# Selective scan: sums kept by columns, and running sums added by VectorE as it empties the bank

## The chip, the cores and the metric

The kernel runs on one core of one Trainium2 chip. A core has five engines that run their own instruction streams and wait for one another through semaphores: TensorE (PE; its weight loads are listed apart as PEld), VectorE (DVE), ScalarE (ACT), GpSimd (POOL) and SyncE (SP), which here only issues DMAs. The metric is the time of one execution on the device in microseconds; less is better. All data are float32.

## The reference

The model has two layers on an input x of shape (4, 384, 32, 32), that is 4 batches of 384 channels on a 32 x 32 picture.

Layer 0 normalises x in 32 groups of channels and runs a selective scan over the pixels in four directions k: 0 by rows, 1 by columns, 2 by rows backwards, 3 by columns backwards. Each of the 384 channels has 16 states:

```python
def step(h, inp):
    dtt, ut, bt, ct = inp
    dA = jnp.exp(dtt[..., None] * A)
    h = h * dA + (dtt * ut)[..., None] * bt[:, :, None, :]
    y = jnp.einsum('bkdn,bkn->bkd', h, ct)
    return (h, y)
```

The results of the four directions are added per pixel, those of 1 and 3 after being turned from column order to row order, and so is D * u. A layer norm over channels, a GELU and a residual follow.

Layer 1 turns the picture into 1024 tokens of 384 channels per batch: layer norm, attention with 6 heads in a causal window of 64, a projection, a residual; then a layer norm and a mixture of 4 experts (384 to 1536 to 384, exact GELU), of which each token uses its two best, and a last residual.

## The kernel before, in words

**How the order of the work is made.** The program is written as generators: one for each stage, each yielding one operation after another, or a condition to wait for. The class Machine runs them while the program is built. It keeps a clock for each engine, gives each operation a cost (`Engine.ask`, lines 155 to 199), and always issues the operation that could start first, with a bias: EARLY (-6 us) for the scan's surroundings and attention, LATER (+6 us) for the experts. So the order of the instructions on each engine is fixed when the program is built and follows from these costs; the chip only waits where data are not ready. `Engine.run` issues one operation, `Engine.all` several as one (line 144). For TensorE the costs are stretched by COLD = 1.9[...]; an operation marked `steady` is not stretched. The helpers record almost every instruction under two lines, L142 (single operations) and L153 (those issued together), so the profile is read by the names of tiles.

**The scan.** There are 16 turns: 4 batches, in each the directions 1, 3, 0, 2 (ORDER). A turn has 12 blocks of 32 channels, and a block has 4 groups of 4 states, so that a tile holds 32 channels x 4 states on 128 partitions and 1024 pixels along the free axis: 48 tiles a turn, 768 in all. Two blocks are worked side by side. For each tile:

- `times_b`: GpSimd multiplies dt * u (dts) by B (bc) into a tile z, one of seven;
- `decay`: ScalarE writes dA = exp(dt * A) into one of two tiles in PSUM;
- `scan`: VectorE runs the recurrence (TENSOR_TENSOR_SCAN), in place in dA or into z;
- `times_c`: VectorE (z<-dA,bc) or GpSimd (z<-z,bc) multiplies by C. The planner chooses by which of the two clocks is behind.

**The sum over states, and over directions.** `fold_y` (line 873) is where the change lies. For each pair of blocks it takes a tile yp of 128 x 512 (two blocks x two halves of 32 channels on the partitions, 512 pixels along), loads what the earlier directions have summed so far from ydr in HBM, takes one of three PSUM banks (ps_y), and puts yp into it by a matmul with the identity. Then, for each of the four groups of states, it adds the two z tiles: a matmul with the weights `fold` (128 x 32, adding the four states of each channel) for each half of 512 pixels, so four matmuls, which the profile lists as eight instructions, on four strips of 32 columns of the array. For directions 1 and 3 the z tile is in column order, and the fold reads it so that the result comes out in row order: 32 neighbouring results take every 32nd element of z. ScalarE copies the bank back to yp and it is stored in ydr. There are 96 such calls. z tiles go back to `times_b` when their fold has been issued. The first value in ydr is D * u (yd), written by `normal` in `group_norm`, line 667.

**The rest.** When the 48 folds of all directions of a batch are through, `tokens` does the attention in 8 tiles of 128 tokens, `route` picks experts and gives each token a row, GpSimd scatters the rows by indirect DMA, and `experts` works 19 blocks of 128 rows per batch (76 in all). A block is 36 matmuls ps_hid, 36 GELUs on ScalarE, 12 matmuls y_ff and 3 transposes ps_xb (the profile shows two instructions for each matmul), and loads 8 tiles of weights of 576 KB. `combine` gathers the two rows of a token and adds them. The experts of one batch run beside the scan of the next; those that are not done when the scan of the last batch ends follow after it.

Of the kernel before, what the change touches and what calls it, by code (L numbers as in the profile page):

```python
# [12 lines left out]
AF = mybir.ActivationFunctionType  # L13
ALU = mybir.AluOpType
# [4 lines left out]
B, D, HH, WW = 4, 384, 32, 32  # L19
# [12 lines left out]
NG = NS // SG  # L32
# [78 lines left out]
class Op:  # L111


    def __init__(self, eng, outs, ins, cost, table, size):
        self.eng, self.outs, self.ins, self.cost, self.table, self.size = eng, outs, ins, cost, table, size
        self.work = 0.0
        self.steady = False


TABLES = {AF.Exp: "exp", AF.Ln: "ln", AF.Gelu: "gelu", AF.Sqrt: "sqrt"}  # L120
# [10 lines left out]
class Engine:  # L131
# [12 lines left out]
    def all(self, calls):  # L144

        asked = [self.ask(*c) for c in calls]
        outs, ins = ([ap for o in asked for ap in getattr(o, side)] for side in ("outs", "ins"))
        whole = Op(self.name, outs, ins, sum(o.cost for o in asked), None, 0)
        whole.work = sum(o.work for o in asked)
        whole.steady = asked[-1].steady  # L150
        yield whole
        for op, a, k in calls:
            getattr(self.real, op)(*a, **k)  # L153

    def ask(self, op, a, k):
        aps = [v for v in list(a) + [v for n, v in k.items() if n not in ("out", "accum_out")] if hasattr(v, "tensor")]
        if "out" in k:
            outs, ins = [k["out"]], aps
        else:
            outs, ins = aps[:1], aps[1:]  # L160
        if op == "value_load":
            outs, ins = [], aps
        if op == "tensor_tensor_reduce":
            outs, ins = outs + ins[-1:], ins[:-1]
        if k.get("accum_out") is not None:
            outs = outs + [k["accum_out"]]
        for v in list(k.values()):
            if isinstance(v, bass.IndirectOffsetOnAxis):
                ins = ins + [v.ap]
        n = max(v.free_size() if callable(v.free_size) else v.free_size for v in (outs if op == "matmul" else outs + ins))  # L170
        size, table = 0, None
        if "dma" in op:
            size = max(_nbytes(v) for v in outs + ins[:1])
            if op == "indirect_dma_start":
                size = P * D * 4
            cost = dict(pool=1.0, act=0.38, sp=0.48)[self.name]
        elif self.name == "pe":
            cost = max(n, 90) * (0.00088 if op == "transpose" else 0.00176)
            if outs[0].shape[0] == 32:
                cost = 0.108 + 0.000417 * n  # L180
            if ins[0].shape[0] < 32:
                cost *= 0.6
        elif self.name == "act":
            cost = 0.08 + 0.00085 * n + 0.1 * sum(hasattr(k.get(v), "tensor") for v in ("bias", "scale"))
            cost += 0.19 if "accum_out" in k else 0.0
            table = TABLES.get(a[2]) if op == "activation" else None
        elif self.name == "pool":
            cost = 0.1 + 0.0022 * n
        elif self.name == "sp":
            cost = 1.5  # L190
        else:
            cost = 0.17 + 0.00198 * n if "scan" in op else 0.14 + 0.00105 * n
            if n < 256 and not any(v.space == PSUM for v in outs + ins):
                cost += 0.5
        asked = Op(self.name, outs, ins, cost, table, size)
        if self.name == "pe":
            asked.steady = outs[0].shape[0] == 32
            asked.work = cost * min(ins[0].shape[0], P) / P if outs[0].shape[0] > 32 else 0.5 * cost
        return asked


def _nbytes(ap):
    n = 4
    for s in ap.shape:
        n *= s
    return n
# [6 lines left out]
class Machine:  # L213
# [50 lines left out]
    def account(self, op, start):  # L264
        e = op.eng
        if op.table and op.table != self.table:
            start += TABLE_LOAD
            self.table = op.table
        end = start + op.cost
        if e == "pe":  # L270

            left, end = op.cost, start
            while left > 0:
                n = int(end / WINDOW)
                f = 1.0 if op.steady or self.worked.get(n - 1, 0.0) > WINDOW / 3 else COLD
                step = min(left * f, (n + 1) * WINDOW - end + 1e-6)
                self.worked[n] = self.worked.get(n, 0.0) + op.work * step / f / op.cost
                left, end = left - step / f, end + step
        self.busy[e] += end - max(self.clock[e], start)
        self.clock[e] = end  # L280
        if op.size:
            self.dma = max(self.dma, end) + op.size / DMA_RATE
            end = max(end + DMA_TIME, self.dma + 1.0)
            e = "dma"
        for aps, log, w in ((op.ins, self.read, False), (op.outs, self.written, True)):
            for ap in aps:
                name = ap.tensor.name
                if str(ap.space) .endswith("DRAM"):
                    self.dram.setdefault(name, []).append((*self.span(ap), end, w))
                elif log.get(name, (0.0, None))[0] <= end:  # L290
                    log[name] = end, e
        self.reach = max(self.reach, end)
# [80 lines left out]
WINDOW, COLD = 3.413, 1.9  # L373
# [5 lines left out]
def conv_attn_hybrid(  # L379
# [29 lines left out]
    ident = const.tile([P, P], F32, name="ident")  # L409
# [5 lines left out]
    dsum = const.tile([P, T], F32, name="dsum")  # L415
    nc.vector.tensor_reduce(dsum, ds_sb.rearrange("p k t -> p t k"), AX.X, ALU.add)

    fold = const.tile([P, 32], F32, name="fold")
# [55 lines left out]
    with tc.tile_pool(name="setup", bufs=1) as setup:  # L474
# [15 lines left out]
        for j in range(JB):  # L490
            ps = banks.now("ps_al")
# [44 lines left out]
    pwl = dram.tile([P, T * D], F32, name="pwl", bufs=1)  # L536

    ORDER = (1, 3, 0, 2)
    turns = [(b, ORDER[ki]) for b in range(B) for ki in range(KG)]
    blocks = [(i, t, j) for i in range(len(turns)) for t in range(T) for j in range(JB)]  # L540
    NSLOT = len(blocks) * NG
# [7 lines left out]
    pe, act, dve, pool, sp = m.pe, m.act, m.dve, m.pool, m.sp  # L549
# [65 lines left out]
    def group_norm(b):  # L615
# [17 lines left out]
        g = rp.tile([P, 5, T], F32, tag="g", name="g", bufs=1)  # L633
# [3 lines left out]
        ps = yield from banks.take("ps_gm", 0)  # L637
        for n, src in enumerate((mean, dev)):
            for t in range(T):
                yield from pe.matmul(  # L640
                    ps[:GROUPS, T : T + 1], gm[:, t, :], src[:, t : t + 1],
                    start=t == 0, stop=t == T - 1,
# [16 lines left out]
        def normal(t):  # L659
            u = yield from us_.take("un")  # L660
            yield from sp.dma_start(u, x[b, ts(t, P)].rearrange("p h w -> p (h w)"))
            yield from act.activation(
                u, u, AF.Identity, bias=g_off[:, t : t + 1], scale=g_rstd[:, t : t + 1]
            )
            yield from sp.dma_start(udr[b][t], u)
            yd = yield from zs_.take("yd")
            yield from act.activation(yd, u, AF.Copy, scale=dsum[:, t : t + 1])
            us_.give(u)
            for j in range(JB):
                yield from sp.dma_start(  # L670
                    ydr[b][t, j].rearrange("(q d) l -> d q l", q=2),
                    yd[32 * j : 32 * j + 32, :].rearrange("d (q l) -> d q l", q=2),
                )
            zs_.give(yd)
# [198 lines left out]
    def fold_y(n):  # L873


        i, t, j = blocks[n]
        b, k = turns[i]
        rows_y = ydr[b][t, j : j + 2].rearrange("j r l -> (j r) l")
        prev = yield from yps.take("yp")
        yield from sp.dma_start(prev, rows_y)  # L880
        ps = None
        for g in range(NG):
            s = n // 2 * SP + 2 * g
            yield lambda: s in ready and s + 1 in ready
            pair = zs[s], zs[s + 1]
            yield m.settled(*pair)
            mm = Calls()
            if ps is None:
                ps = yield from banks.take("ps_y", 0)
                mm.matmul(ps, ident, prev, start=True, stop=False)  # L890
            for n_z, z in enumerate(pair):
                for h in range(2):
                    if k % 2:
                        rhs = z.rearrange("p (w h) -> p h w", h=HH)[:, ts(h, HH // 2), :]
                    else:
                        rhs = z[:, ts(h, LH)]
                    q = 32 * (2 * n_z + h)
                    mm.matmul(ps[q : q + 32, :], fold, rhs, start=False, stop=g == NG - 1)
            yield from pe.all(mm)
            zs_.give(zs.pop(s), zs.pop(s + 1))  # L900
        yield from act.copy(prev, ps)
        banks.give(ps)
        yield from sp.dma_start(rows_y, prev)
        yps.give(prev)
        folded[b] = folded.get(b, 0) + 2
        if folded[b] == KG * NB:
            have.add(("scan", b))
# [601 lines left out]
```

## Time and profile before

| | |
|---|---|
| three runs, median (lowest to highest) | 4246.56 us (4246.25 to 4254.88) |
| profiled execution | 4255.8 us |
| its span, first to last instruction | 4254.0 us |
| mean granted TensorE clock | 0.819 |
| busy PE, DVE, ACT, POOL | 3377.0, 2852.8, 2373.1, 2813.7 us |
| first scan, last fold, end | 103, 3175, 4254 us |
| fold matmuls / identity matmuls (instructions) | 3072, mean 914 ns / 192, mean 814 ns |
| copies yp<-ps_y on ScalarE | 96, mean 584 ns |

The page gives the busy time of each engine over the whole span, which is a sum over stages that have different limits; the view by windows gives the same for stretches of time. A line of a group reads: source line, engine, operation, output<-inputs, shapes, count, busy time, mean duration of one in ns, then the idle time of the engine just before them and what ended it. In a timeline a line gives the start in us, the duration in us, the engine, the source line, the operation and how many were merged; what stands in brackets is the idle time before it. PEclk is the clock that TensorE was granted, 1.0 being full speed.

### The profile page before, as it was taken

The numbers are of one execution on the slowest core, as the hardware profiler recorded it, in microseconds if no ns is written. First come the engines' busy times: TensorE is split into PE (matmuls) and PEld (weight loads), VectorE is DVE, ScalarE is ACT, GpSimd is POOL, SyncE is SP. The second block draws the span as 40 slices with busy tenths as digits, with TensorE's granted clock in tenths as the row PEclk, the third lists the DMA queues.
The fourth block names the chain that finished last, engine by engine and source line by source line (L and its number), as shares of the span: only waits on it lengthen the run. The fifth ranks groups of instructions, "written<-read, shape, count | busy, mean of one in ns | idle before, by whom it ended". The sixth has DMA issues, their size and how long they took to land. (4 is left out here: it accounts for less than half of the span.)

```text
span 4254.0 us, 50073 instructions
## 1 busy us (share of the span) xinstructions
PE 3377.0 (79%) x16222; PEld 1952.7 (46%) x16222; DVE 2852.8 (67%) x2995; ACT 2373.1 (56%) x3961; POOL 2813.7 (66%) x1468
## 2 busy tenths in 40 slices
PE   2556555588875987978788787887899999999997
PEld 1000110144441553534445343444567777887875
DVE  2999999987888978888888888888861222001001
ACT  2555455666655887777677767677663443222221
POOL 1999989997897899988878889898871001101001
PEclk7655665687875998878788887887899999999997
DMA  6566563542446985635668846556577438998995
GB/s 210 200 239 230 202 227 127 177 150 107 150 145 240 365 326 189 221 124 195 211 232 293 297 149 205 187 189 216 176 248 260 138 103 301 355 319 294 313 319 165
DMA packets 368573, 935.16 MB, mean 220 GB/s; under 512 B 48372, under 2 KB 160120, under 8 KB 368312
## 3 DMA queue, kind: packets, MB, share of 16 engines
q1 hardware_dynamic: 360120, 906.79, 61.3%
q0 software_dynamic: 8192, 25.17, 1.7%
q8 instruction: 129, 2.11, 0.2%
q14 instruction: 132, 1.08, 0.1%
HBM read 786.39 MB, written 164.30 MB: 223 GB/s over the span
## 5 line engine op out<-in xcount | busy, mean ns | idle before, releaser
L142 POOL TENSOR_TENSOR z<-dts,bc 128x1024 f32<-128x1024 f32 x768 | 1796.2, 2364 | 236.5 <-PE ps_y L153 136.9
L142 ACT ACTIVATE dA<-dts,a 128x1024 f32<-128x1024 f32 x768 | 853.1, 1118 | 488.6 <-DVE z L142 467.6
L153 PE MATMUL ps_y<-z,fold 128*32 128x512 f32 x3072 | 827.1, 914 | 320.8 <-DVE z L142 162.8
L142 DVE TENSOR_TENSOR_SCAN dA<-dA,z 128x1024 f32<-128x1024 f32 x414 | 947.3, 2288 | 111.1 <-ACT dA L142 92.1
L142 POOL TENSOR_TENSOR z<-z,bc 128x1024 f32<-128x1024 f32 x354 | 831.1, 2360 | 101.0 <-DVE z L142 100.1
L142 DVE TENSOR_TENSOR_SCAN z<-dA,z 128x1024 f32<-128x1024 f32 x354 | 795.7, 2276 | 55.7 <-ACT dA L142 53.1
L153 PEld LDWEIGHTS ps_hid<-xbt,w_sb 128*128 128x128 f32 x5472 | 683.4, 201 | 136.5 <-issue 22.4
L153 PE MATMUL ps_hid<-xbt,w_sb 128*128 128x128 f32 x5472 | 702.0, 286 | 40.7 <-ACT dt L142 16.4
L153 PE MATMUL y_ff<-w_sb,hs 128*128 128x384 f32 x1824 | 664.4, 503 | 14.3 <-ACT hs L142 7.9
L142 ACT ACTIVATE hs<-ps_hid,bb 128x128 f32<-128x128 f32 x912 | 271.9, 366 | 542.2 <-PE ps_hid L153 417.3
L142 DVE TENSOR_TENSOR z<-dA,bc 128x1024 f32<-128x1024 f32 x414 | 505.9, 1222 | 23.3 <-PE ps_y L153 0.5
L153 PEld LDWEIGHTS ps_y<-z,fold 128*32 128x32 f32 x3072 | 93.9, 122 | 800.7 <-POOL z L142 336.5
L142 ACT ACT_TABLE_LOAD x340 | 436.2, 1283 | 12.0 <-PE ps_g L153 5.8
L153 PEld LDWEIGHTS y_ff<-w_sb,hs 128*128 128x128 f32 x1824 | 333.4, 196 | 228.0 <-issue 40.3
L142 POOL DMA_INDIRECT cb<-ysdr,idx x64 | 61.8, 966 | 548.8 <-DMA cb<-t2dr 269.7
L153 POOL TENSOR_TENSOR rn<-rn,half 128x1 f32<-128x1 f32 x96 | 52.6, 548 | 288.6 <-DVE rn L153 286.6
L142 DVE COPY xbt<-ps_xb 128x384 f32<-128x384 f32 x40 | 22.2, 556 | 329.2 <-PE ps_xb L153 329.2
L153 PE MATMUL ps_y<-yp,ident 128*128 128x512 f32 x192 | 139.1, 814 | 90.0 <-ACT yp L142 20.9
L142 POOL DMA_INDIRECT xsdr<-tks,idx x64 | 63.7, 995 | 208.5 <-DMA xsdr<-tks,idx 151.3
L153 PE MATMUL ps_o<-v,pt 128*128 128x64 f32 x720 | 160.1, 345 | 6.1 <-ACT dt L142 2.3
L142 DVE COPY yb<-y_ff 128x384 f32<-128x384 f32 x27 | 15.0, 556 | 214.4 <-PE y_ff L153 205.1
L153 PEld LDWEIGHTS ps_o<-v,pt 128*128 128x128 f32 x720 | 130.1, 228 | 43.7 <-ACT dt L142 4.0
(187 smaller groups left out, 3480.3 us busy)
## 6 DMA issues: line engine op xcount, KB each, us to landing
w_sb<-wl SPq DMA_DIRECT2D x608, 576.0 KB
dts<-dtr SPq DMA_DIRECT2D x384, 512.0 KB
bc<-xdr SPq DMA_DIRECT2D x128, 512.0 KB
ub<-udr SPq DMA_DIRECT2D x48, 512.0 KB
dtr<-e SPq DMA_DIRECT2D x48, 512.0 KB
dtr<-dt SPq DMA_DIRECT2D x48, 512.0 KB
yp<-ydr SPq DMA_DIRECT2D x96, 256.0 KB
ydr<-yp SPq DMA_DIRECT2D x96, 256.0 KB
```

What stands on the lines that cost most here:

```text
L142: return getattr(self.real, op)(*a, **k)
L153: getattr(self.real, op)(*a, **k)
```

## The change

The sums in ydr are kept in column order for as long as directions 1 and 3 run, and yp no longer goes through TensorE.

- `normal` writes the first yd in column order: ScalarE reads u by columns and writes yd contiguously, as two halves of 16 rows, each by columns.
- For directions 1 and 3 the fold reads z as it lies: of each picture column a run of 16 pixels (a half of the picture) and then the next column's run. The result is in column order.
- The first matmul of the bank is now that of the first group (start where g == 0), not the identity.
- After the last group VectorE adds the bank to yp, into yp, instead of ScalarE's copy.
- In direction 3, the last by columns, ScalarE then writes yp back into the bank in row order and copies the bank to yp, so that directions 0 and 2 and `tokens` find row order. This holds for 24 of the 96 calls.
- In the planner the mark `steady` goes, the cost of a fold matmul is 0.01 + 0.00022 n instead of 0.108 + 0.000417 n (for n = 512: 0.123 us instead of 0.321), stretched by COLD like any other, and several operations issued together take the activation table of the first that has one. The planner's new costs change the order of instructions on every engine.

```diff
 class Op:
         self.work = 0.0
-        self.steady = False
...
     def all(self, calls):
-        whole = Op(self.name, outs, ins, sum(o.cost for o in asked), None, 0)
+        table = next((o.table for o in asked if o.table), None)
+        whole = Op(self.name, outs, ins, sum(o.cost for o in asked), table, 0)
         whole.work = sum(o.work for o in asked)
-        whole.steady = asked[-1].steady
...
             if outs[0].shape[0] == 32:
-                cost = 0.108 + 0.000417 * n
+                cost = 0.01 + 0.00022 * n
...
         if self.name == "pe":
-            asked.steady = outs[0].shape[0] == 32
...
-                f = 1.0 if op.steady or self.worked.get(n - 1, 0.0) > WINDOW / 3 else COLD
+                f = 1.0 if self.worked.get(n - 1, 0.0) > WINDOW / 3 else COLD
...
     ORDER = (1, 3, 0, 2)
+    LAST_BY_COLUMNS = 3
...
         def normal(t):
-            yield from act.activation(yd, u, AF.Copy, scale=dsum[:, t : t + 1])
+            yield from act.activation(
+                yd.rearrange("p (q w h) -> p q w h", q=2, w=WW),
+                u.rearrange("p (q h w) -> p q w h", q=2, w=WW), AF.Copy, scale=dsum[:, t : t + 1],
+            )
...
     def fold_y(n):
             if ps is None:
                 ps = yield from banks.take("ps_y", 0)
-                mm.matmul(ps, ident, prev, start=True, stop=False)
             for n_z, z in enumerate(pair):
                 for h in range(2):
                     if k % 2:
-                        rhs = z.rearrange("p (w h) -> p h w", h=HH)[:, ts(h, HH // 2), :]
+                        rhs = z.rearrange("p (w h) -> p w h", h=HH)[:, :, ts(h, HH // 2)]
                     else:
                         rhs = z[:, ts(h, LH)]
                     q = 32 * (2 * n_z + h)
-                    mm.matmul(ps[q : q + 32, :], fold, rhs, start=False, stop=g == NG - 1)
+                    mm.matmul(ps[q : q + 32, :], fold, rhs, start=g == 0, stop=g == NG - 1)
             yield from pe.all(mm)
             zs_.give(zs.pop(s), zs.pop(s + 1))
-        yield from act.copy(prev, ps)
+        yield from dve.tensor_tensor(prev, ps, prev, ALU.add)
+        if k == LAST_BY_COLUMNS:
+            yield from act.copy(
+                ps.rearrange("p (h w) -> p w h", w=WW), prev.rearrange("p (w h) -> p w h", w=WW)
+            )
+            yield from act.copy(prev, ps)
         banks.give(ps)
```

## The prediction

> **What bounds the kernel now.** I read the summary by stages first, because a busy share over the whole span mixes stages with different limits. The window view gives the busy time of each engine in each stretch, then the granted TensorE clock, the DMA share and GB/s:
>
> ```profile
> core 0: us, PE busy (x) PEld busy (x) DVE busy (x) ACT busy (x) POOL busy (x), PEclk, DMA share, GB/s
> ...
> 103.00:770.00 667.00, 376.56 (x920) 57.66 (x918) 646.88 (x431) 355.93 (x399) 616.54 (x268) 0.61 0.58 206
> 770.00:3175.00 2405.00, 1932.00 (x9057) 1062.53 (x9053) 2028.81 (x2047) 1688.42 (x2641) 2091.80 (x1052) 0.82 0.59 207
> 3175.00:3622.00 447.00, 435.21 (x2666) 345.11 (x2665) 105.00 (x377) 159.72 (x437) 46.66 (x79) 0.96 0.62 207
> 3622.00:4194.00 572.00, 566.00 (x3419) 450.46 (x3418) 35.25 (x67) 132.97 (x435) 29.73 (x31) 0.99 0.90 313
> ```
>
> There are two regimes. From the first scan (103) to the last fold (3175), VectorE and GpSimd share the pace: together they are busy 5384 us of 2 x 3072, or 87.6%. In batch 0 VectorE alone is at 97%. After 3175 VectorE and GpSimd have almost nothing left and TensorE is at 97 to 99%: the **tail** is TensorE's, and every expert block that the scan stage has not done is paid there in full. A ten-block stretch of the tail gives its price:
>
> ```profile
> 3622.20:3783.30 161.10, 161.10 (x993) 129.31 (x992) 11.15 (x20) 35.35 (x120) 14.55 (x15) 1.00 0.97 341
> ```
>
> PE is busy all of it, so a block of 128 token rows costs 16.1 us there. Last, the groups of instructions, which give the prices, and the waits in the scan stage:
>
> ```profile
> L142 POOL TENSOR_TENSOR z<-z,bc 128x1024 f32<-128x1024 f32 x354 | 831.1, 2360 | 101.0 <-DVE z L142 100.1 <-PE ps_y L153 0.2
> L142 DVE TENSOR_TENSOR z<-dA,bc 128x1024 f32<-128x1024 f32 x414 | 505.9, 1222 | 23.3 <-PE ps_y L153 0.5
> L153 PE MATMUL ps_y<-yp,ident 128*128 128x512 f32 x192 | 139.1, 814 | 90.0 <-ACT yp L142 20.9 <-ACT hs L142 15.4 <-ACT yl L142 13.9
> L142 ACT COPY yp<-ps_y 128x512 f32<-128x512 f32 x96 | 56.1, 584 | 72.0 <-PE ps_y L153 70.2 <-DMA bc<-xdr 1.5
> L142 DVE TENSOR_TENSOR e<-ps_sp,ub x96: 682/844/1056, 83.0 to 2967.2; 128x512 f32<-128x512 f32 x96
> ...
> POOL z L142 <- PE ps_y L153: 134.3, 59, 9.4
> ```
>
> The last line is GpSimd's own list from 770 to 3175: it stands 134.3 us because TensorE, in order, has not yet folded the z that would free its buffer. In the same stretch VectorE waits 142 us for TensorE (o<-ps_o 63.0, s<-ps_s 35.1 and smaller) and 142 us for the dA of ScalarE.
>
> [...] By columns, the fold reads z with a step of 32 floats[...]; a burst is the 8 instructions that fold a pair of z:
>
> ```profile
> 2902.97 1.07 PE L153 MATMUL ps_y<-z,fold 128*32 128x512 f32 x8
> 1854.60 1.90 PE L153 MATMUL ps_y<-z,fold 128*32 128x512 f32 x8
> 293.19 1.92 PE L153 MATMUL ps_y<-z,fold 128*32 128x512 f32 x4 [1.61 <-DVE z L142]
> 645.50 1.92 PE L153 MATMUL ps_y<-z,fold 128*32 128x512 f32 x4 [1.79 <-DVE z L142]
> ```
>
> By rows (2902.97) 1.07, by columns (1854.60) 1.90. The two last lines are batch 0, by columns and by rows: both 1.92. [...] PEclk is 0.61 there, and at that clock the order of reading costs nothing. [...]
>
> **The change, part by part.** Besides the diff I use the instruction order of the built program, which the planner's new costs rearrange.
>
> 1. *Identity matmuls out.* 96 pairs, 139.1 us of TensorE's busy time, all in the scan stage. The load of yp still runs (same DMAs, same queue), but what waits for it is now the add at the end, when it has long landed.
>
> 2. *Runs of 16.* Half of the turns (k = 1 and 3) read by columns; two of these eight are in batch 0, cold, and win nothing. Six turns x 24 bursts x (1.90 - 1.07) = 120 us of TensorE. I take the row price; the bounds are 1.07 and 1.90.
>
> 3. *The add on VectorE.* 96 x 0.69 us (between 0.682 above and the 0.688 and 0.700 medians of the other 128x512 adds on PSUM) = +66 us of VectorE. ScalarE loses 96 x 0.584 = 56 us and gets 48 copies for k = 3, half of them reading by columns: 24 x 0.58 + 24 x (0.58 to 1.12, the fast and slow form of xo<-ps_x) = 28 to 41 us. The initial yd, 12 x 1.14, may double, +14 at most, off the path: ScalarE is at 53 to 70% there.
>
> 4. *A new wait in VectorE's queue.* The add waits for the last fold burst. ScalarE met that wait in 36 of 96 cases, 70.2 us. Behind the add stand the next scan and times_c, and behind these ScalarE's dA. VectorE mostly has a 2.3 us scan ahead of the add, which covers a burst; I take half, 35 us; bounds 0 and 70.
>
> 5. *The rearranged order.* Multiplications by C on VectorE fall from 414 to 398 and on GpSimd rise from 354 to 370: -16 x 1.222 = -20 us and +16 x 2.360 = +38 us. Table loads rise from 340 to 368, +36 us on ScalarE at 1.283. The largest shift: after the last fold, ps_hid matmuls fall from 1719 to 1467 (252, at 36 a block 7 blocks), y_ff from 579 to 492 (87, at 12 a block 7 and a quarter), ps_xb from 141 to 120 (21, 7 blocks). **Seven expert blocks move from the tail into the scan stage.** Everything else after the last fold is the same.
>
> *Tail:* 7 x 16.1 = -113 us. The cover is kept: after the last routing 28 blocks remain (34 before), 19 of the last batch, so 9 x 16.1 = 150 us stand for the scatters, which took 105 us after the routing matmuls (3610 to 3715).
>
> *Scan stage:* (a) VectorE +66 - 20 = +47 and GpSimd +38, 85 us on two engines that share the pace at 87.6%: 85 / (2 x 0.876) = +48. (b) TensorE: -139 - 120 + 113 = -146 us. Of the 277 us that VectorE and GpSimd wait for it I take 80 away; half counts for the pace: -40 (bounds 0 and -100; that TensorE's queue is filled anew speaks for little). (c) The new wait, half of 35: +20 rounded up. (d) Last turn: 297 ps_hid instead of 153, four blocks, 64 us more on a TensorE busy 172 of 193 us, which becomes warmer as it fills: +10 (bounds 0 and +40). Sum +38, bounds about -50 and +110.
>
> *Together* -113 + 38 = -75. The profiled execution took 4255.8 us (span 4254.0): 4181. The median of the three runs, 4246.56, lies 9 us lower: **4172 us**.
>
> **Rivals.** *TensorE was the brake of the scan stage.* For it: the 277 us above, and nearly 150 us less work. With the relief at its bound, -100 for -40, the time is 4112. Against: in batch 0 VectorE is at 97% and waits for nothing, and the blocks fill the queue again.
>
> *The runs are no faster* (the change does not do what it says). TensorE then falls by 26 us only and the relief by that share, to -7: 4205. Against: the price by rows, already seen.
>
> *Slower: VectorE stands behind the fold.* Place: the add at the end of fold_y, at the head of VectorE's queue, with TensorE in order behind expert matmuls. If VectorE alone sets the pace, all of ScalarE's 70 us moves over and nothing is relieved: -113 + 47 + 70 + 10 = +14, or 4261. It decides from (113 + 8.5 - 47 - 10) / 96 = 0.67 us of wait per add; ScalarE's mean is 0.73. For it: VectorE did stand 5.95 us for ps_o at 2930. Against: the burst it waits for is shorter, and the scan ahead covers it.
>
> **How the numbers follow.** The sum as worked out, within 40 us of 4172: 0.60. TensorE the brake, 4095 to 4132: 0.17. Runs no faster, or several costs near their upper bounds, 4212 to 4238: 0.10. Slower: 0.09. Near no change: 0.04. About 0.2% (8.5 us) is what a measurement of this kernel can tell from none. Range 4095 to 4240, which leaves out the slower case and most of no change.
>
> **What would show it.** Right: the last fold between 3150 and 3260; from it to the end about 965 us instead of 1079, still at 16.1 a block; warm bursts by columns near 1.07; no identity group; yp<-ps_y,yp on VectorE near 0.69. Wrong: VectorE waiting for ps_y over 65 us in all, a scan stage longer by over 110 us, bursts at 1.90, or a gap in TensorE's tail before the last batch.

## The result, and the profile after

The changed kernel takes 4188.24 us (median of 4 runs, 4181.22 to 4198.25) against 4250.72 us before: a ratio of 0.9849, 95% interval 0.9815 to 0.9883, or 62 us less. The forecast was 4172, which is 75 us less than the median it started from. The profiled execution has a span of 4190.3 us.

The window view of the changed kernel, cut at its first scan (105), its last fold (3231) and its end:

```profile
core 0: us, PE busy (x) PEld busy (x) DVE busy (x) ACT busy (x) POOL busy (x), PEclk, DMA share, GB/s
105.00:3231.00 3126.00, 2215.94 (x10473) 1186.61 (x10472) 2716.60 (x2573) 2093.41 (x3096) 2746.41 (x1344) 0.75 0.62 216
3231.00:4190.00 959.00, 920.88 (x5495) 730.65 (x5490) 139.83 (x441) 276.33 (x818) 83.14 (x116) 0.95 0.74 250
```

The same view of the kernel before, for its scan stage (103 to 3175):

```profile
103.00:3175.00 3072.00, 2308.56 (x9973) 1120.19 (x9971) 2675.69 (x2477) 2044.35 (x3040) 2708.34 (x1319) 0.77 0.59 207
```

The scan stage is 54 us longer and the tail 120 us shorter. VectorE has 41 us more to do in the scan stage and GpSimd 38; together they are busy 87.4% of it, as they were before (87.6%). A block in the tail still costs 16.1 us; another window of the changed kernel, with the columns of the first, holds eight of them, TensorE without a gap:

```profile
3653.90:3782.80 128.90, 128.90 (x795) 103.52 (x794) 4.46 (x8) 32.14 (x104) 14.39 (x15) 1.00 0.98 358
```

The groups of the changed kernel that answer to those shown of before, with the folds of before ahead of them. The identity group is gone; ScalarE's copies out of the bank have become VectorE's adds:

```profile
L153 PE MATMUL ps_y<-z,fold 128*32 128x512 f32 x3072 | 827.1, 914 | 320.8 <-DVE z L142 162.8 <-POOL z L142 157.5
...
L152 PE MATMUL ps_y<-z,fold 128*32 128x512 f32 x3072 | 732.7, 800 | 531.3 <-POOL z L141 269.2 <-DVE z L141 172.7 <-ACT dt L141 30.8
L141 DVE TENSOR_TENSOR yp<-ps_y,yp 128x512 f32<-128x512 f32 x96 | 65.6, 683 | 72.4 <-PE ps_y L152 71.1 <-DMA yp<-ydr 0.8 <-DMA w_sb<-wl 0.3
L141 POOL TENSOR_TENSOR z<-z,bc 128x1024 f32<-128x1024 f32 x370 | 867.4, 2355 | 128.6 <-DVE z L141 118.7
L141 DVE TENSOR_TENSOR z<-dA,bc 128x1024 f32<-128x1024 f32 x398 | 486.1, 1221 | 12.9
L141 ACT ACTIVATE yd<-un,dsum 128x1024 f32<-128x1024 f32 x12 | 24.7, 2065 | 0.3 <-PE ps_y L152 0.2
```

Read the line of the adds first: 683 ns an add, as priced, but 71.1 us of standing in front of the 96 adds for the bank, where the prediction had put 35. The folds take 94 us less than before (733 for 827). Why not 120 is seen in the timeline of TensorE, in bursts by columns of batch 2 (the first two lines) and one by rows of batch 0:

```profile
1701.88 1.06 PE L152 MATMUL ps_y<-z,fold 128*32 128x512 f32 x8
1785.38 1.94 PE L152 MATMUL ps_y<-z,fold 128*32 128x512 f32 x8 [10.80 <-ACT dt L141]
647.87 1.93 PE L152 MATMUL ps_y<-z,fold 128*32 128x512 f32 x8 [4.90 <-POOL z L141]
```

A run of 16 is read as fast as a row was before, 1.06 us a burst for 1.07, at a granted clock of 1.00 in both (windows cut at the bursts). But after an idle stretch of 10.80 us a burst takes 1.94, and one by rows in batch 0 takes 1.93, both at 0.50. At that clock the runs gain next to nothing: in batch 0 a whole burst by columns takes 1.93 us in the changed kernel (at 309.55) and took 1.96 before (at 273.68), both at 0.50. The granted clock of the scan stage is 0.75, against 0.77 before.

The waits of the scan stage in the changed kernel, VectorE's longest (total us, times, longest):

```profile
DVE dA L141 <- ACT dA L141: 94.0, 70, 6.0
DVE o L141 <- PE ps_o L152: 69.4, 22, 6.3
DVE yp L141 <- PE ps_y L152: 66.5, 42, 6.8
```

(The other 4.6 us of the 71.1 are those of the very last add, behind the last fold.)

And GpSimd's longest wait, before (103 to 3175) and after:

```profile
POOL z L142 <- PE ps_y L153: 137.1, 62, 9.4
...
POOL z L141 <- PE ps_y L152: 155.8, 58, 9.1
```

GpSimd waits 156 us for folds, 137 before. Summed over the whole list, VectorE waits 212 us for TensorE in the scan stage instead of 146. So the relief that the prediction counted on isn't to be seen here, although TensorE's busy time in the stage fell by 93 us.

### The profile page after: what moved, and what is told of

Same layout as the page of the kernel before. It is cut to its first block, busy times and chain, and to the rows that moved or that the text cites. A ratio compares the mean times of both kernels' runs of the same rounds, so it can differ in the third digit from the quotient of the medians.

```text
span 4190.3 us, 49613 instructions
## 1 busy us (share of the span) xinstructions
PE 3169.3 (76%) x16030; PEld 1930.3 (46%) x16030; DVE 2882.8 (69%) x3068; ACT 2403.3 (57%) x3952; POOL 2844.5 (68%) x1484
## 5 line engine op out<-in xcount | busy, mean ns | idle before, releaser
L152 PE MATMUL ps_y<-z,fold 128*32 128x512 f32 x3072 | 732.7, 800 | 531.3 <-POOL z L141 269.2
L141 DVE TENSOR_TENSOR_SCAN dA<-dA,z 128x1024 f32<-128x1024 f32 x398 | 910.5, 2288 | 101.5 <-ACT dA L141 94.0
L141 POOL TENSOR_TENSOR z<-z,bc 128x1024 f32<-128x1024 f32 x370 | 867.4, 2355 | 128.6 <-DVE z L141 118.7
L141 DVE TENSOR_TENSOR_SCAN z<-dA,z 128x1024 f32<-128x1024 f32 x370 | 832.0, 2276 | 25.5 <-ACT dA L141 24.3
L152 PE MATMUL ps_hid<-xbt,w_sb 128*128 128x128 f32 x5472 | 710.5, 288 | 44.1 <-ACT dt L141 17.5
L141 DVE TENSOR_TENSOR z<-dA,bc 128x1024 f32<-128x1024 f32 x398 | 486.1, 1221 | 12.9
L152 PE MATMUL ps_p<-ident,s 128*128 128x128 f32 (+1 forms) x528 | 104.9, 328 | 47.7 <-ACT dt L141 21.1
L152 PE MATMUL ps_dt<-xd,dtw_sb 12*128 12x512 f32 x192 | 97.5, 858 | 43.9 <-ACT dt L141 19.4
```

The costliest lines, as they stand in the source:

```text
L141: return getattr(self.real, op)(*a, **k)
```

## The experiments

The theory at the start was that VectorE and GpSimd share the pace of the scan stage, that TensorE's load there is nearly free, and that the gain is the seven blocks that leave the tail (theory 1). The rival was that TensorE's time in the scan stage counts (theory 2). All runs stand in this table; stages and waits are read from one profiled execution each, "waits" being those of VectorE and of GpSimd for TensorE in the scan stage, added up; "blocks" is how many expert blocks, counted by their ps_hid matmuls, leave the tail. The kernel before was measured again beside each set of runs; its medians lay between 4251 and 4254 us, and each ratio is to the one beside it. Where an expectation names 372 us of waits, it means the 370 of the change.

| run | blocks | scan stage | tail | TensorE busy in the stage | waits | median | ratio to before (95%) |
|---|---|---|---|---|---|---|---|
| before | 0 | 3072 | 1079 | 2309 | 283 | 4251 to 4254 | |
| the change | 7 | 3126 | 959 | 2216 | 370 | 4188 | 0.9849 (0.9815 to 0.9883) |
| x1 costs alone | 5.75 | 3150 | 988 | 2376 | 395 | 4233 | 0.9959 (0.9944 to 0.9975) |
| x2 old costs | 2.75 | 3073 | 1044 | 2165 | 284 | 4212 | 0.9899 (0.9864 to 0.9934) |
| x3 strided, same order | 7 | 3158 | 956 | 2294 | 421 | 4222 | 0.9934 (0.9918 to 0.9950) |
| x4 second add, same order | 7 | 3144 | 955 | 2207 | 345 | 4209 | 0.9904 (0.9870 to 0.9938) |
| x5 identity back, same order | 7 | 3171 | 961 | 2293 | 434 | 4238 | 0.9962 (0.9952 to 0.9972) |
| x6 add later | 2.75 | 3120 | 1036 | 2180 | 307 | 4261 | 1.0021 (1.0010 to 1.0032) |
| x7 small pieces | 5 | 3148 | 1004 | 2217 | 390 | 4247 | 0.9994 (0.9983 to 1.0004) |
| x8 runs alone | 0.5 | 3075 | 1076 | 2184 | 293 | 4262 | 1.0018 (1.0007 to 1.0029) |
| x9 add alone | 3.5 | 3084 | 1024 | 2238 | 270 | 4223 | 0.9918 (0.9887 to 0.9948) |
| x10 fold cost measured | 1.5 | 3048 | 1049 | 2147 | 256 | 4196 | 0.9857 (0.9829 to 0.9884) |
| x11 fold cost lower | 5.75 | 3147 | 996 | 2224 | 377 | 4244 | 0.9979 (0.9970 to 0.9988) |
| x12 small costs too | 0.5 | 3034 | 1096 | 2121 | 247 | 4233 | 0.9951 (0.9932 to 0.9970) |

### x1: the planner's costs alone

```diff
 (from the kernel before)
-                cost = 0.108 + 0.000417 * n
+                cost = 0.01 + 0.00022 * n
...
-                f = 1.0 if op.steady or self.worked.get(n - 1, 0.0) > WINDOW / 3 else COLD
+                f = 1.0 if self.worked.get(n - 1, 0.0) > WINDOW / 3 else COLD
```

The planner stretches a cost by COLD where it has given TensorE little work just before; the second part of the edit ends the exception for folds.

> The kernel before with nothing but the planner's new costs for the fold (0.123 us for 0.321, stretched when cold); every matmul, copy and add is as before. Multiplications by C stay 414 on VectorE and 354 on GpSimd; 5.75 expert blocks move from the tail into the scan stage. Theory 1 (VectorE and GpSimd share the pace of the scan stage and TensorE's load there is nearly free, so the gain is the blocks that move): tail -5.75 x 16.1 = -93, scan stage 0 to +15, time 4155 to 4175, faster than the changed kernel. Theory 2 (TensorE's load in the scan stage counts, and the runs of 16 and the lost identity pay for the blocks): TensorE gets 93 us more on top of the slow folds, scan stage +50 or more, time 4205 or more.

The tail is 91 us shorter, as both theories say. The scan stage in the window view:

```profile
104.00:3254.00 3150.00, 2375.98 (x10532) 1180.19 (x10530) 2682.19 (x2493) 2101.49 (x3125) 2717.63 (x1326) 0.78 0.60 212
```

It is 78 us longer, with nearly the same work on VectorE and GpSimd (2682 and 2718 us busy). Theory 1 fails: the new costs bring 19 us of the 62. Shared out over the blocks that is 78 / 5.75 = 13.6 us in the scan stage for each, against 16 saved in the tail; but it is the price of the blocks together with the rest of the new order, not of a block alone. The new rule on activation tables is not in this run, and it stays in x2 and x8; no run tries it by itself.

### x2: the change with the planner's costs of before

The reverse edit in the changed kernel, with `steady` restored.

> The changed kernel with the planner's costs of before: runs of 16, sums by columns and the add on VectorE as in the change, but only 2.75 blocks leave the tail. Multiplications by C: 395 on VectorE, 373 on GpSimd. Theory 1: tail -44; work of VectorE 66 - 23 = +43 and of GpSimd +45, 88 / (2 x 0.875) = +50 in the scan stage: about 4255, no gain at all. Theory 2: TensorE has 259 us less of its own work and gets back 44, so the scan stage grows little or shrinks: 4190 to 4215.

4212, at the upper end of what theory 2 gave, and 39 us of the 62. The tail is 35 us shorter; the stage is as long as before in spite of 63 us more work on VectorE and GpSimd together (2703 and 2744 us). So in this order what the parts save on TensorE about pays for the work that they add elsewhere.

### x3: strided reads, in the order of the changed kernel

```diff
-                        rhs = z.rearrange("p (w h) -> p w h", h=HH)[:, :, ts(h, HH // 2)]
+                        rhs = z.rearrange("p (w h) -> p h w", h=HH)[:, ts(h, HH // 2), :]
```

> The changed kernel with its order of instructions kept, but in directions 1 and 3 the fold reads z with a step of 32 again, as before (the sums of these directions come out in another order of pixels, so the output is not the reference's). It puts back the 120 us of TensorE alone. Theory 1: 0 to +15 us on the changed kernel. Theory 2: +35 to +100 us.

+33 us of the median, all of it in the scan stage (3158). The group of the folds in x3:

```profile
L152 PE MATMUL ps_y<-z,fold 128*32 128x512 f32 x3072 | 834.6, 920 | 516.3 <-POOL z L141 264.2 <-DVE z L141 161.9 <-ACT dt L141 28.8
```

102 us more than in the changed kernel, for 33 us of time: 0.3 us a us. As the order is the same to the instruction, this is the price of strided reads in this order. It is twice what theory 1 allowed, and just below theory 2's range.

### x4: a second add

```diff
         yield from dve.tensor_tensor(prev, ps, prev, ALU.add)
+        nc.vector.tensor_tensor(ps, ps, prev, ALU.add)
```

> The changed kernel with its order kept and, right behind each of the 96 adds, a second add of the same size into the bank, which the planner doesn't know of (for direction 3 and the others it changes nothing that is read later). +66 us of VectorE in the scan stage, nothing else. Theory 1 (VectorE and GpSimd share the pace): +66 / (2 x 0.875) = +38 us. VectorE alone sets the pace: +66 to +76. VectorE's idle time takes it: 0 to +10.

+21 us (the intervals of the two ratios still overlap). The scan stage:

```profile
105.00:3249.00 3144.00, 2206.93 (x10473) 1180.02 (x10472) 2771.99 (x2667) 2094.25 (x3096) 2747.04 (x1344) 0.75 0.61 214
```

VectorE is busy 55 us longer in the stage (2772) and stands idle 37 us less; its waits for dA, for one, fall from 118 to 105 us. So it does not set the pace alone. Between the other two expectations the run does not decide: 21 lies halfway between the 10 of idle time and the 32 that a shared pace makes of 55 us (38 of 66).

### x5: the identity put back

```diff
                 ps = yield from banks.take("ps_y", 0)
+                nc.tensor.matmul(ps, ident, prev, start=True, stop=False)
...
-                    mm.matmul(ps[q : q + 32, :], fold, rhs, start=g == 0, stop=g == NG - 1)
+                    mm.matmul(ps[q : q + 32, :], fold, rhs, start=False, stop=g == NG - 1)
```

> The changed kernel with its order kept, and the identity matmul of yp put back in front of each bank's first fold, unknown to the planner (yp then counts twice, so the output is not the reference's). It puts 96 x 1.07 us or a little more, some 105 to 140 us, back on TensorE. If TensorE's time in the scan stage costs what the strided reads showed (33 us for about 120, 0.27 a us), +28 to +38 us. If only what stands before the last fold of a bank counts, since the identity comes at its start, 0 to +10.

The group of the identity in x5:

```profile
L893 PE MATMUL ps_y<-yp,ident 128*128 128x512 f32 x192 | 140.4, 821 | 121.0 <-ACT dt L141 28.3 <-DMA yp<-ydr 18.2 <-ACT yl L141 17.5
```

+50 us, more than the 28 to 38 expected. The scan stage:

```profile
104.00:3275.00 3171.00, 2292.87 (x10666) 1204.14 (x10666) 2712.65 (x2573) 2093.93 (x3097) 2748.24 (x1345) 0.77 0.61 213
```

TensorE is busy only 77 us longer in it, not 140: the same folds take 703 us instead of 733, at a granted clock of 0.77 for 0.75. A second part of the price is 18.2 us of standing for the load of yp, which in the changed kernel only the add needs, at the end. How long the identity stands for this load changes with the order: 5.4 us in the kernel before, 17.3 in x1. So what the change takes off TensorE is worth about 33 + 50 us in its own order, if the two add up, which no run tried.

### x6: the add held back in the plan

```diff
+        end = m.written[ps.tensor.name][0]
+        yield lambda: m.t >= end + LAG      # LAG = 1.5
         yield from dve.tensor_tensor(prev, ps, prev, ALU.add)
```

> The changed kernel with the planner holding the add back until 1.5 us after it believes the fold to end, so that VectorE takes up something else first. The order moves: only 2.75 blocks leave the tail, as with the old costs; multiplications by C 396 and 372. VectorE's wait for the bank falls from 71 us to under 25. If that wait costs half of itself, as the prediction took it, the scan stage is 20 to 25 us shorter than that of the run with the old costs (3073), time 4185 to 4195. If the wait only stands where VectorE would otherwise stand for ScalarE or GpSimd, the stage is 3065 to 3080 and the time about 4212.

The wait in front of the add is nearly gone (12.6 us), and nothing is won: 4261 us, against 4212 in x2 with as many blocks moved. VectorE's list of waits for x6's scan stage shows others in its place:

```profile
DVE o L141 <- PE ps_o L152: 63.5, 21, 6.4
DVE s L141 <- PE ps_s L152: 42.2, 33, 5.7
...
DVE dA L141 <- POOL z L141: 24.6, 20, 3.6
```

The wait for ps_s is 42.2 (24.5 in the changed kernel), and that for z from GpSimd 24.6. Neither expectation holds: the stage is 3120, not 3065 to 3080. As the whole order moved, this does not price the wait; it shows only that this way of planning it away brought no gain.

### x7: expert blocks in pieces of 0.64 us

`hidden` and `output` issue the matmuls of each j by themselves instead of three j together.

> The changed kernel with the planner allowed to put other work between the three parts of an expert's 9 ps_hid matmuls (1.9 us) and of its 3 y_ff matmuls (1.9 us): pieces of 0.64 us. 5 blocks leave the tail instead of 7. Theory: what moved blocks cost in the scan stage is that folds and attention stand behind their long strings on TensorE; then VectorE's and GpSimd's waits for TensorE fall from 372 us to under 300 and the time to 4160 to 4180. If not the strings but the mere amount of TensorE work counts, it lies between the run with the old costs (4212) and the changed kernel (4188), at 4195 to 4205.

4247, outside both. Waits for TensorE are 390 us, not under 300. So shorter pieces did not shorten the waits. As the planner made another order of them, with 5 blocks moved, the run does not clear the long strings for good.

### x8 and x9: one part alone, with the planner's costs of before

x8 is the change with the old costs, the identity and `act.copy(prev, ps)` in place of the add; x9 is the kernel before with the add and without the identity.

> One part alone: sums by columns and runs of 16, with the planner's costs of before, the identity and ScalarE's copies kept (and two more copies in direction 3). Half a block leaves the tail; multiplications by C 416 and 352, as before. TensorE has 120 us less. By the price of the strided reads: -33 us, and -4 for the half block: 4212 to 4220, which would be all that the parts gain without the new costs. If runs only pay together with the blocks that they make room for: 4235 to 4250.

> The other part alone: the add on VectorE and no identity, with the planner's costs of before, strided reads and row order throughout. 3.5 blocks leave the tail; multiplications by C 395 and 373. If freed time of TensorE pays by itself (50 us for the identity, by the run that put it back), against 30 to 50 us for the work of VectorE and GpSimd and 13 us gained on the blocks: 4215 to 4240. If it pays only where the planner has filled it, as the runs alone suggest: 4255 to 4280.

x8 takes 4262 us, above both of its ranges: the runs alone bring nothing. TensorE is busy 124 us less in the scan stage (2184), yet the stage is 3075 and GpSimd, in its list of waits of x8's scan stage, stands longer for folds than before:

```profile
POOL z L142 <- PE ps_y L154: 156.5, 47, 12.2
```

Why is not shown. The old costs plan a burst at 1.29 us; by columns it took 1.90 and now takes 1.06, so part of what is freed lay above the plan and found no use either. ScalarE's 48 further copies and 17 more table loads (52 us more busy in the stage) muddy this run. x9, the add alone, takes 4223, in the range for freed time of TensorE that pays by itself. Its ratio is 0.9918, and that of both parts with the old costs (x2) 0.9899, with overlapping intervals: under the old costs the runs add nothing that shows.

### x10 and x11: the fold's cost, to either side

```diff
-                cost = 0.01 + 0.00022 * n
+                cost = 0.01 + 0.00041 * n      # x10;  x11: 0.00015
```

> The changed kernel with a fold cost that fits a warm burst as measured (0.22 us for 512 columns, 0.88 a burst, for 0.123), stretched when cold. Only 1.5 blocks leave the tail; multiplications by C 396 and 372. If a block that stays in the tail costs 16.1 there and saves the 12.5 us that blocks cost in the scan stage: 4188 + 5.5 x 3.6 = 4208, tail 1055, stage about 3070. If an honest cost of the fold makes the static order fit the chip better: waits for TensorE below 280 us, stage under 3050, time 4190 or less. Over 4230: neither, the arrangement itself decides.

> The changed kernel with a fold cost of 0.087 us for 512 columns instead of 0.123. 5.75 blocks leave the tail instead of 7; multiplications by C 406 and 362. By the price of a block: 4188 + 1.25 x 3.6 = 4193. More than 20 us off that: two orders with nearly the same contents differ by what no price of a part tells.

The 0.88 of the first expectation is what a further burst adds: in the changed kernel two without a pause take 1.92 us at a granted clock of 1.00 (at 1619.88), one 1.06.

x10 decides whether the seven blocks are needed. One and a half leave the tail, and the time is the same within what can be told (4196; intervals nearly alike). The stage and the waits fell as an honest cost of the fold was to make them, the time not quite (4190 or less). Its scan stage in the window view:

```profile
105.00:3153.00 3048.00, 2147.04 (x9912) 1116.12 (x9911) 2703.57 (x2524) 2045.66 (x2996) 2740.75 (x1334) 0.74 0.59 210
```

The wait of GpSimd for folds in that stretch:

```profile
POOL z L141 <- PE ps_y L152: 95.6, 50, 8.2
```

And that of VectorE for the bank:

```profile
DVE yp L141 <- PE ps_y L152: 47.3, 31, 3.7
```

Here the relief is plain: the stage is 24 us shorter than before although VectorE and GpSimd have 60 us more to do, and GpSimd's wait for folds is 96 us instead of 137. The tail gives the other 30 us of the gain. x11 moves almost as many blocks as the change, with almost the same contents, and at 4244 it is 55 us slower (stage 21 longer, tail 37 longer), far from the 4193 that the price of a block gave.

### x12: TensorE's small operations planned as measured

```diff
-            cost = max(n, 90) * (0.00088 if op == "transpose" else 0.00176)
+            cost = max(n, 120) * 0.00176
```

> The run with the fold's measured cost, and besides the planner's costs of TensorE's small operations set to what the trace shows warm: 0.211 us for any of up to 120 columns, transposes included (it had 0.113 for a transpose and 0.158 for the 64 columns of ps_o; measured 0.218 and 0.214). Half a block leaves the tail; multiplications by C 391 and 377. If orders planned with truer costs wait less: waits of VectorE and GpSimd for TensorE under 256 us, scan stage 3020 to 3040, which makes up for the block that stays: 4180 to 4195. If the stage does not get below 3048, the tail's 16 us for the block are simply lost: 4210 or more.

The scan stage is 3034 and the waits 247, the least of all, as expected; but the tail is 47 us longer than in x10 for one more block, and the time is 4233. So the forecast of the stage holds and that of the time, 4180 to 4195, does not. Of the 30 us of the tail that the block does not explain, some is attention that now falls behind the last fold (21 ps_o and 18 ps_pr<-ot,wp instructions more than in x10); the rest was not followed. None of the runs beats the change clearly; x10 equals it.

## Why the prediction was right or wrong

*The tail, -113:* right, -120. Seven blocks at 16.1, and the cover for the scatters held (9 x 16.1 is 145 us, not 150, which changes nothing): TensorE stands idle 38 us in the tail, 41 before.

*Identity, runs, add, yd:* the instructions and prices came out: 0.683 us an add, 1.06 us a warm burst (at a granted clock of 1.00), yd nearly doubled at 2065 ns (1143 before). That a run of 16 has the price of a row was the author's estimate; the 1.06 bears it out. All 96 adds take 665 to 694 ns beside a GpSimd that is busy 88% of the scan stage, and z<-z,bc on GpSimd takes 2355 ns, 2360 before: the times show neither slowed by the other. The runs were worth 94 us of TensorE instead of 120. The prediction took batch 0 alone as cold (1.92 us) and the six later turns by columns as warm throughout. In the changed kernel 59 of their 144 bursts still take 1.7 us or more; before, 47 of the 144 bursts by rows of the same batches did, so most of this was there already. Two readings were off without harm. The lines of batch 0 in the prediction are halves of bursts (x4); a whole one takes as long there, 1.93 us. And of the copies for k = 3 half write the bank by columns, none reads by columns; they take 588 ns, the low end of the range given.

*The new wait, 35:* the term was mis-sized; it is 71, just over the upper bound of 70, and over the 65 us that the prediction had named as a sign of being wrong. But VectorE's idle time in the stage rose by 13 us only (3126 - 2717 = 409, against 3072 - 2676 = 396): its waits for ScalarE's dA fell from 145 to 118 and those for GpSimd's z as well. The point of 0.67 us a call, from which the wait was to decide, was passed (0.74) and the kernel did not get slower, so that rival's premise, that VectorE alone sets the pace, was wrong; x4 shows it directly.

*The relief, -40, and the blocks, the step that failed:* the prediction netted the seven blocks against the freed TensorE time at one price and took 80 us off the waits for TensorE. They rose by 87 instead, from 283 to 370. Its price was 40 / 146 = 0.27 us a us, which makes -71 of the 259 us freed and +31 of the 113 us put on. For what was freed the runs give nearly that: 33 us (x3) and 50 us (x5), about -83. What was put on costs far more than 4.4 us a block: 13.6 by x1, 12.5 from x2 to the change and 14 from x10 to the change (78 us of scan stage for 5.5 blocks), or about +95 for seven, against 16 saved for each.

These three are differences between replanned orders, and two other pairs give 1 (x6 to the change) and 23 (x10 to x11), so the size is uncertain. Taken at these sizes, the stage's +54 is -83 and +95, with +42 left over for the work and the wait on VectorE and GpSimd and for the last turn, where the prediction had 78; no run measured that remainder. The total came out close by luck: a relief of -40 that was about +12 was made up by the other terms and by 7 us more in the tail. That the gain needs the seven blocks is refuted by x10, which reaches 4196 with one and a half.

*Last turn, +10:* not seen; from its first scan to the last fold it takes 202 us, as before, though TensorE is busy 195 of them instead of 180, at a granted clock of 0.98 instead of 0.87.

*The rivals.* That TensorE was the brake of the scan stage comes nearest to the truth in its cause, though not in its time: x3 and x5 put time back on TensorE alone and lengthen the stage by 32 and 45 us. In the table, too, the stage is longer where the waits for TensorE are, from 3034 at 247 us to 3171 at 434, with exceptions such as x6. It is not the only brake, since x4's delay of VectorE costs 21 us. That runs are no faster is refuted by the timeline (1.06 us a warm burst by columns, 1.90 before).

What stays open is why orders with nearly equal contents differ by 50 us (the change and x11; x2 and x6). That limits every comparison of replanned kernels here, x1 and x10 among them; only x3, x4 and x5, whose order is that of the change, price a part by itself. How much of the 62 us is owed to the parts, and how much to an order that happened to fit, is therefore not settled.

## What to carry to other kernels

Where a planner fixes the order, price a part by editing it behind the planner's back, in an order kept to the instruction; a replanned kernel mixes the part with a new arrangement, worth up to 50 us here. Work moved out of a stage that one engine fills, into a stage where that engine has idle time, need not be free: count what it delays, in three comparisons of orders here 12 to 14 of the 16 us saved on a block. And a new wait on an engine is to be read with the idle time of that engine as a whole, since it may only take the place of another.

## What the runs showed of the hardware that was not expected

- For ScalarE a step of 32 floats costs nothing in ps_y<-yp, where it lies in PSUM (128 x 512, read from SBUF as it lies and written into the bank by columns: 588 ns, against 584 for the contiguous copy out). It costs nearly double where it lies in SBUF: in yd<-un, which reads by columns (128 x 1024: 2065 ns against 1143). The two differ in size and operation as well, and no run tells these apart.

```profile
L141 ACT COPY ps_y<-yp 128x512 f32<-128x512 f32 x24 | 14.1, 588 | 8.7 <-DVE yp L141 8.5
```

- Taking work off TensorE lowered the clock that it was granted: 0.796 in the changed kernel, against 0.810 and 0.811 with the strided reads (x3) or the identity (x5) put back in the same order. In x5 the same folds take 703 us instead of 733.
